# Keys' squares behind the next group's copies, gathers ahead of the attention's first key loads, one root per norm, full last key chunks

## The chip, the cores and the metric

One core of one Trainium2 chip runs the kernel. The core has a matmul engine (TensorE, PE), a vector engine (VectorE, DVE), a scalar engine (ScalarE, ACT), a general engine (GpSimd, POOL) and SyncE (SP), which here only issues DMA transfers; POOL issues DMA transfers too. Each engine runs its instructions in order and waits on semaphores for the others. The metric is the device time of one execution in microseconds (us), lower is better.

## The reference

Eight sequences of 100 tokens with 512 features (`x`) go through four layers, each added to `x`; each has its own context of 722 rows.

```python
x = x + _L0_xattn_ref(ctx_1024, _layernorm(x))     # time warping: sums of context rows along the path
x = x + _L0_ffn_ref(_layernorm(x), ...)            # 16 experts, the best 3 per token
x = x + _L1_xattn_ref(ctx_1024, _layernorm(x), mask_BxS2_bk0, ...)
x = x + _L1_ffn_ref(_layernorm(x), ...)            # 4 experts over one base product, 2 per token
```

What the change touches is the third layer. It norms its input once more, takes keys and values from the context's 722 rows and from the 100 tokens, and scales each head's query and key to unit root mean square:

```python
xn = layernorm(x, ln_x_g, ln_x_b)                  # x: the context, 722 rows
ln = layernorm(latents, ln_l_g, ln_l_b)            # latents: _layernorm(x), 100 rows
q = ln @ W_q
kv = jnp.concatenate([xn @ W_kv, ln @ W_kv], axis=1)
k, v = (kv[..., :INNER], kv[..., INNER:])          # to 8 heads of 64
qn = rmsnorm(q, q_gamma) * SCALE
kn = rmsnorm(k, k_gamma)
sim = jnp.einsum('bhid,bhjd->bhij', qn, kn)
sim = jnp.where(full_mask[:, None, None, :], sim, neg)   # tokens' keys are never masked
attn = jax.nn.softmax(sim, axis=-1)
out = jnp.einsum('bhij,bhjd->bhid', attn, v) @ W_out + b_out
```

Here `rmsnorm` divides by `max(norm / sqrt(64), 1e-8)`. The latents are a layer norm of a layer norm: with variance v and e = 1e-5, the factor of both together is 1 / sqrt(v / (v + e) + e) x 1 / sqrt(v + e).

## The kernel before

All arithmetic is in float32. A scheduler puts each engine's instructions in order, from the program's order and its own estimates, unless the program says otherwise (`tc.manual_schedule` keeps the program's own order for the engines it names, `tc.issue_after` puts instructions behind a given one).

The 800 tokens are rows in seven tiles of 128 (`NT`, the last of 32). Stages in order of time, with the span's us from the trace:

*Distances, time warping, path (0 to 403).* DVE runs the wavefront of the cost matrix, and then 100 steps of the path (L440), each over a row loaded back from `step_d`. L448 makes the selector `sel`, and `pf` (L453) on PE spreads the path over partitions. Then `pe` (L483) sums context rows (`cr`) along the path.

*Context keys and values (121 to 606, beside all that).* The context's 722 rows per sequence are six chunks of 128, in two groups of three: 16 groups, 48 chunks. `products(b, ct, c0)` (the first of two functions with that name) makes, for each chunk, `pk` and `pv` (L720, four fp32 matmuls each, of 512 columns, two passes each), ACT copies them with a scale per row to `k` (L724) and `vr` (L726), and POOL adds a bias to `k` (L725). Then, for the whole group, ACT takes 24 squares with a running sum (L737, eight heads of three chunks) and one root (L740) into `rk`. `keys` of the group before (`behind`) follows: DVE limits and inverts `rk` (L746, L747), POOL multiplies (L750), PE transposes (`ptk`, L754), ACT copies to `kt` (L755), and POOL issues the store to `k_d` (L757); the values' stores to `v_d` are issued by POOL at L728 and L733. All PSUM tiles here (`pk`, `pv`, `ptk` and those ahead of the loop) share one ring of four banks with the tag `mm`. There are two buffers of `k`, `vr` and `rk` and one of `kt`.

*Route and experts (488 to 946).* The router's products `pt`, `pl` end at 529.4, DVE computes places (with `pw` from PE in between, L571), POOL issues 21 indirect stores of rows to `xs_d` from 561.6 to 588.3, PE and DVE add the experts' output biases (`po` L673, `X` L674). Then 16 expert slots: `xr` loads, `px` transposes (L796), `xe` copy (L798), `ph` (L807), `py` (L822), and `rows_out`, whose last store to `ys_d` POOL issues at 946.55. The pools of the keys' stage are closed ahead of the experts'.

*Spill branch (near 946 to 961).* `tc.If(some > 0)` holds work for tokens that found no place. With these inputs it is not taken, but all engines meet there. `load(b)` for the attention issues, on SP, the context's keys of a sequence (`akt`, L910, 1444 KB), the mask row (`mw`, L912); ACT makes `mb` from it (L915). `early` loads two sequences ahead of the queries, and a third load comes from the attention's loop.

*Queries (961 to 1091).* For each token tile, POOL gathers three expert rows (`back`, L978, indirect, four buffers), DVE adds them (L982), then takes the statistics (L988, L989), and the norm of the norm with two roots on ACT (L992, L995) and reciprocals and products on DVE (L993 to L998), then `xn` (L1000). PE transposes (`pt` L1003), multiplies (`pqk` L1013, `apv` L1049), DVE norms per head (L1017 to L1022), PE transposes again (`apt`), ACT makes `qt` and `kl`, and SP stores `kl` to `k_d` (L1041) and loads the tokens' columns of the early keys (`tokens`, L924). From tile 2 on the first sequence's `scores` (`psc` L933) and `largest` (L943) run too.

*Attention (1091 to 1300).* A sequence has 822 keys, the 722 of the context and the 100 tokens, in seven chunks that start at `STARTS`; the sixth has 82 rows, the seventh 100 (`key_rows`). For each of the four head pairs and two groups of chunks (`KG`, four and three) PE makes `pst` (L1113), DVE adds the negated maximum (L1123), ACT takes the exponentials with the mask as a bias per row (`mk`, L1129), PE multiplies with the values (`apo` L1141), POOL adds the weights over chunks (`two`, `ws`, L1153 to L1160), PE spreads their sums (`pws` L1167) and DVE inverts (`rs` L1174). `va` holds the values (L1099, L1103, five loads a sequence).

*Last feed-forward (1300 to 1536)* on PE.

Of the kernel before, what the change touches and what calls it, by code (L numbers as in the profile page):

```python
# [33 lines left out]
MW = (S2 + 3) // 4  # L34
# [11 lines left out]
KW = S2 + KP  # L46
STARTS = (0, 128, 256, 384, 512, 640, S2)
# [11 lines left out]


def key_rows(c):
    return (*STARTS, KEYS)[c + 1] - STARTS[c]

# [6 lines left out]
def kernel(  # L70
# [47 lines left out]
    nc.vector.tensor_scalar_mul(qgs, gcol[:, 0:1], DH ** -0.5)  # L118

# [382 lines left out]
    if True:  # L502
# [178 lines left out]
        for half, dst in ((0, kbias), (1, vbias)):  # L681
            pb = kps.tile([P, D], F32, tag="mm", name="kvb")
            for dc in range(DC):
                nc.tensor.matmul(
                    pb, lncol[:, 1, dc : dc + 1].to_broadcast([P, P]), wc[:, dc, half * D : (half + 1) * D],
                    start=dc == 0, stop=dc == DC - 1,
                )
            nc.scalar.copy(dst, pb)
        pb = kps.tile([P, D], F32, tag="mm", name="kvc")
# [10 lines left out]
        for half in range(2):  # L700
            pb = kps.tile([P, D], F32, tag="mm", name="kvm")
# [7 lines left out]
        def products(b, ct, c0):  # L709

            k = kvp.tile([P, 3, D], F32, tag="k", name="k")
            vr = kvp.tile([P, 3, D], F32, tag="vr", name="vr")
            rk = kvp.tile([P, 3, NH], F32, tag="rk", name="rk")
            for c in range(c0, c0 + 3):
                rs = crstd[:, b, c : c + 1]
                pk = kps.tile([P, D], F32, tag="mm", name="pk")
                pv = kps.tile([P, D], F32, tag="mm", name="pv")
# [8 lines left out]
                nc.scalar.mul(vr[:, c - c0, :], pv, rs)  # L726
# [4 lines left out]
            if c0 > 0:  # L731
                for r0, r1 in ((0, RLAST // 16 * 16), (RLAST // 16 * 16, RLAST)):
                    nc.gpsimd.dma_start(out=v_d[b, (RC - 1) * P + r0 : (RC - 1) * P + r1, :], in_=vr[r0:r1, 2, :])  # L733
            junk = kvp.tile([P, DH], F32, tag="kjunk", name="kjunk", bufs=1)
            for c in range(3):
                for h in range(NH):
                    nc.scalar.activation(  # L737
                        junk, k[:, c, h * DH : (h + 1) * DH], AF.Square, accum_out=rk[:, c, h : h + 1]
                    )
            nc.scalar.activation(rk, rk, AF.Sqrt, scale=1.0 / DH)  # L740
            return b, c0, k, rk

        def keys(b, c0, k, rk):

# [3 lines left out]
            for c in range(3):  # L748
                kh = k[:, c, :].rearrange("p (h d) -> p h d", h=NH)
                nc.gpsimd.tensor_tensor(kh, kh, rk[:, c, :].unsqueeze(2).to_broadcast([P, NH, DH]), ALU.mult)  # L750
                ptk = kps.tile([P, D], F32, tag="mm", name="ptk")
# [8 lines left out]
        for b in range(B):  # L760
# [3 lines left out]
            for c0 in range(0, RC, 3):  # L764
                now = products(b, ct, c0)
                if behind is not None:
                    keys(*behind)
# [126 lines left out]
    if True:  # L894
# [8 lines left out]
        if True:  # L903
            ak = attn.enter_context(tc.tile_pool(name="attnk", bufs=2, side="right"))

            def load(b):

                kt = ak.tile([P, NPAIR, KW], F32, tag="akt", name="akt", bufs=3)
                nc.gpsimd.memset(kt[:, :, KEYS:], 0.0)
                nc.sync.dma_start(out=kt[:, :, :S2], in_=k_d[b, :, :, :S2])  # L910
# [3 lines left out]
                nc.gpsimd.memset(mb[:, S2:], 0.0)  # L914
                nc.scalar.activation(mb[:, :S2], mw.bitcast(U8)[:, :S2], AF.Copy, bias=-FMAX, scale=FMAX)  # L915
# [6 lines left out]
            def tokens(st):  # L922

                nc.sync.dma_start(out=st["kt"][:, :, S2:KEYS], in_=k_d[st["b"], :, :, S2:])  # L924
# [41 lines left out]
            early = [load(b) for b in range(2)]  # L966
            with tc.tile_pool(name="qkv", bufs=2, side="right") as qp:
                nc.sync.dma_start(out=wo, in_=w_out.rearrange("(c p) n -> p c n", p=P))
                nc.sync.dma_start(out=bo, in_=b_out.partition_broadcast(P))
                eps = qp.tile([P, 1], F32, name="eps", bufs=1)  # L970
                nc.gpsimd.memset(eps, EPS)
                given = 0
                for t in range(NT):
                    n = tok_rows(t)
                    cols = ds(t * P, n)
                    for k in range(TOPK):
                        back = qp.tile([P, D], F32, tag="back", name="back", bufs=4)
                        nc.gpsimd.indirect_dma_start(  # L978
# [11 lines left out]
                    rr = qp.tile([P, 4], F32, tag="rr", name="rr")  # L990
                    one, var, two, shift = (rr[:, i : i + 1] for i in range(4))
                    nc.scalar.activation(one, mv[:, 1:2], AF.Sqrt, bias=eps)  # L992
                    nc.vector.reciprocal(one, one)  # L993
                    nc.vector.scalar_tensor_tensor(var, mv[:, 1:2], one, one, ALU.mult, ALU.mult)
                    nc.scalar.activation(two, var, AF.Sqrt, bias=eps)  # L995
# [500 lines left out]
```

## Time and profile before

| what | value |
|---|---|
| median of 3 runs | 1538.27 us (1536.83 to 1538.72) |
| profiled execution, its own time | 1538.33 us |
| its span | 1536.6 us |
| mean granted TensorE clock | 0.949 |
| PE busy | 1385.6 us, 90% of the span |
| DVE, ACT, POOL busy | 684.9, 485.2, 436.1 us |
| PE busy 121 to 596 in L720 | 191.9 + 176.1 us |
| DMA | 217.78 MB, mean 142 GB/s |

The page gives busy time over the whole span; which engine sets the time differs by stage, so one reads a stage's window first, then what ended PE's idle time in it:

```profile
sum 1152.00, PE 1063.07 PEld 712.35 DVE 366.53 ACT 316.03 POOL 306.61; mean PE 75.93 PEld 50.88 DVE 26.18 ACT 22.57 POOL 21.90
```

This is the last line of the table of windows from 385 us to the end: of 1152 us PE is busy 1063, so 89 us of PE's idle time lie there. In a line of the groups, the figures after the bar are busy us and the mean ns of one instruction, then the idle us just before such an instruction, with the releaser of most of it. In a timeline line the bracket gives the idle time before and what released it.

### The profile page before, as it was taken

To read this page: it belongs to the slowest core of one execution; us is meant where nothing else is said; L and a number is where in the kernel's file an instruction comes from. 1 tells how busy PE (TensorE), PEld (TensorE's weight loads), DVE (VectorE), ACT (ScalarE), POOL (GpSimd) and SP (SyncE) were. 2 spreads that over 40 slices of the span, in tenths; PEclk is the share of its full clock that TensorE was granted. 3 is DMA by queue.
4 is the path that set the end of the run, shared out by engine and by line. 5 is a ranking of instruction groups with operands and counts; after the bars stand their busy time and mean duration, and the time that the engine had idled before them with its cause. 6 is when DMAs were issued, how large, how long until landed. Compare 5 with 4: busy or idle time off the path is not lost. (4 is left out here: it accounts for less than half of the span.)

```text
span 1536.6 us, 19541 instructions
## 1 busy us (share of the span) xinstructions
PE 1385.6 (90%) x7043; PEld 870.6 (57%) x7043; DVE 684.9 (45%) x1492; ACT 485.2 (32%) x1506; POOL 436.1 (28%) x552
## 2 busy tenths in 40 slices
PE   5979887989799998999999996499999997899998
PEld 4443333444333543899999995144476765544433
DVE  3579999799723251101100100634477773322220
ACT  3424354554522554121122221132354543200000
POOL 1014333545423356000000000600365554322210
PEclk8989899999999998899999998699899999999999
DMA  9861213542655143866567786521544420400000
GB/s 307 298 169 38 78 51 109 167 122 71 207 169 158 56 163 139 291 245 237 204 228 250 260 291 237 143 48 35 194 139 133 134 89 1 164 0 0 1 23 21
DMA packets 120857, 217.78 MB, mean 142 GB/s; under 512 B 47765, under 2 KB 49077, under 8 KB 120629
## 3 DMA queue, kind: packets, MB, share of 16 engines
q1 hardware_dynamic: 103413, 152.54, 30.9%
q0 software_dynamic: 16464, 61.44, 11.5%
q10 hardware_dynamic: 880, 2.51, 0.5%
q8 instruction: 58, 0.95, 0.3%
q14 instruction: 42, 0.34, 0.1%
HBM read 163.92 MB, written 50.86 MB: 140 GB/s over the span
## 5 line engine op out<-in xcount | busy, mean ns | idle before, releaser
L720 PE MATMUL pk<-wc,ctk 128*128 128x512 f32 x384 | 191.9, 641 | 25.8 <-ACT vr L726 22.7
L720 PE MATMUL pv<-wc,ctk 128*128 128x512 f32 x384 | 176.1, 597 | 0.0
L807 PE MATMUL ph<-xe,w1t 128*128 128x192 f32 (+4 forms) x1024 | 171.5, 314 | 1.3 <-DVE xe L798 1.3
L822 PE MATMUL py<-hT,w2t 128*128 128x192 f32 (+4 forms) x1024 | 169.7, 310 | 0.0
L807 PEld LDWEIGHTS ph<-xe,w1t 128*128 128x128 f32 x1024 | 154.4, 192 | 4.7 <-DVE xe L798 1.7
L822 PEld LDWEIGHTS py<-hT,w2t 128*128 128x128 f32 x1024 | 153.1, 191 | 1.8
L720 PEld LDWEIGHTS pk<-wc,ctk 128*128 128x128 f32 x384 | 76.9, 205 | 123.6 <-issue 92.8
L737 ACT ACTIVATE kjunk<-k 128x64 f32<-128x64 f32 x384 | 98.0, 255 | 111.3 <-POOL k L725 95.5
L811 ACT ACTIVATE hT<-ph,b1t 128x192 f32<-128x192 f32 (+4 forms) x128 | 51.8, 404 | 253.4 <-PE ph L807 253.4
L720 PEld LDWEIGHTS pv<-wc,ctk 128*128 128x128 f32 x384 | 73.1, 191 | 91.6 <-issue 88.6
L1129 ACT ACTIVATE et<-et,mk 128x200 f32<-128x200 f32 (+2 forms) x224 | 85.8, 451 | 67.2 <-DVE et L1123 67.1
L725 POOL TENSOR_TENSOR k<-k,kbias 128x512 f32<-128x512 f32 x48 | 71.9, 1503 | 99.1 <-ACT k L724 98.9
L798 DVE COPY xe<-px 128x768 f32<-128x768 f32 (+4 forms) x16 | 14.0, 875 | 185.8 <-PE ph L807 170.4
L835 POOL DMA_DIRECT2D ys_d<-yr x28 | 15.3, 547 | 285.8 <-ACT yr L834 285.8
L1356 PE MATMUL fpb<-xT,wi 128*128 128x400 f32 x256 | 91.5, 507 | 1.0 <-DVE z L1378 1.0
L1405 PE MATMUL fpo<-wot,hw 128*128 128x512 f32 x192 | 84.8, 595 | 0.0
L750 POOL TENSOR_TENSOR k<-k,rk 128x512 f32<-128x512 f32 x48 | 63.7, 1353 | 60.2 <-DVE rk L747 60.2
L440 DVE SCALAR_TENSOR_TENSOR junk<-two_i,path,C 8x735 f32<-8x735 f32 x64 | 74.1, 1157 | 9.7 <-DMA C<-step_d 7.7
L1113 PE MATMUL pst<-qt,akt 64*128 64x100 f32 x896 | 66.3, 282 | 6.8 <-DVE et L1123 6.7
L737 ACT ACTIVATION_READ_ACCUMULATOR kjunk<-k 128x1 f32 x384 | 72.0, 188 | 0.0
L1356 PEld LDWEIGHTS fpb<-xT,wi 128*128 128x128 f32 x256 | 47.0, 190 | 42.5 <-issue 9.4
L943 DVE CUSTOM_DVE_ANT_0 junk<-psc,mb 100x822 f32<-100x822 f32 x64 | 64.2, 1003 | 13.6 <-PE psc L933 13.3
(334 smaller groups left out, 2031.3 us busy)
## 6 DMA issues: line engine op xcount, KB each, us to landing
w1t<-in_w SPq DMA_DIRECT2D x16, 2048.0 KB
w2t<-in_w SPq DMA_DIRECT2D x16, 2048.0 KB
ct<-in_context_t SPq DMA_DIRECT2D x8, 1444.0 KB
ctk<-in_context_t POOLq DMA_DIRECT2D x8, 1444.0 KB
akt<-k_d SPq DMA_DIRECT2D x8, 1444.0 KB
cr<-in_context SPq DMA_DIRECT2D x8, 1280.0 KB
va<-v_d SPq DMA_DIRECT2D x8, 1280.0 KB
v_d<-vr POOLq DMA_DIRECT2D x8, 768.0 KB
```

Of the source, the lines that this page charges most:

```text
L440: nc.vector.scalar_tensor_tensor(junk, two_i1, path[:, j + 1 : j + 2], scol, ALU.is_le, ALU.mult, accum_out=path[:, j : j + 1])
L720: nc.tensor.matmul(ps, ct[:, dc, c * P : (c + 1) * P], wc[:, dc, lo : lo + D], start=dc == 0, stop=dc == DC - 1)
L725: nc.gpsimd.tensor_tensor(kc, kc, kbias, ALU.add)
L737: nc.scalar.activation(junk, k[:, c, h * DH : (h + 1) * DH], AF.Square, accum_out=rk[:, c, h : h + 1])
L750: nc.gpsimd.tensor_tensor(kh, kh, rk[:, c, :].unsqueeze(2).to_broadcast([P, NH, DH]), ALU.mult)
L807: nc.tensor.matmul(ph[:, :cap], st["w1t"][:, dc, hc * P : (hc + 1) * P], st["xe"][:, dc, :cap], start=dc == 0, stop=dc == DC - 1,)
L822: nc.tensor.matmul(py[:, dc, :cap], st["w2t"][:, hc, (2 * dh + dc) * P : (2 * dh + dc + 1) * P], st["hT"][:, hc, :cap], start=hc == 0, sto ...
L943: nc.vector.tensor_tensor_reduce(out=junk, in0=ps.rearrange("p b c -> p (b c)")[:S, :KEYS], in1=st["mb"], scale=1.0, scalar=-FMAX, op0=ALU ...
L1113: nc.tensor.matmul(ps[:, i, (c - c0) * S : (c - c0 + 1) * S], st["kt"][rows, hp, STARTS[c] : STARTS[c] + KP], qt[rows, hp, b * S : (b + 1) ...
L1129: nc.scalar.activation(et[:n, c - c0], et[:n, c - c0], AF.Exp, bias=mk[:n, b, c : c + 1])
L1356: nc.tensor.matmul(pb[:, :N2], wi[fc * P // FQ][:, dc, fc * P % FQ : fc * P % FQ + P], xT[:, dc, hh * N2 : (hh + 1) * N2], start=dc == 0, ...
L1405: nc.tensor.matmul(po[:n], hw[:, fc, t * P : t * P + n], wot[:, fc, :], start=fc == 0, stop=fc == FC - 1)
```

## The change

Five edits. (1) The squares and the root move from `products` to `keys`, which runs one group later, and each chunk's eight squares are issued behind the value copy of the same chunk of the next group. `k` gets a third buffer, `pk` and `pv` share three PSUM banks, and `ptk` has one of its own. (2) The two roots of the norm of the norm become one: 1 / sqrt(v (1 + e) + e x e) is the same factor; `eps` becomes a constant, set at the start. (3) The gathers, adds and norm of tile t + 1 come ahead of tile t's products in the program, DVE keeps the program's order there, and the first two key loads move from SP ahead of the branch to POOL's queue, behind the gathers of tiles 1 and 2. (4) The last two key chunks start at 594 and 694 and hold 128 rows each; rows that an earlier chunk has are masked, by the table the host lays out. The work per chunk is then over 128 rows throughout: values in three loads instead of five, the weights' sums in four adds instead of five, and the padding and its memset go. (5) The mask bytes cover the tokens too, so that `mb` is written by one instruction.

```diff
 KEYS = S2 + S
-MW = (S2 + 3) // 4
+MW = (S2 + S + 3) // 4
 KG = ((0, 4), (4, 7))
...
 KP, KC = 128, 7
-KW = S2 + KP
-STARTS = (0, 128, 256, 384, 512, 640, S2)
+STARTS = (0, 128, 256, 384, 512, S2 - KP, KEYS - KP)
 NCH, CW = 15, 49
...
-def key_rows(c):
-    return (*STARTS, KEYS)[c + 1] - STARTS[c]
...
+    eps = const.tile([P, 1], F32, name="eps")
+    nc.gpsimd.memset(eps, EPS * EPS)
...
-            k = kvp.tile([P, 3, D], F32, tag="k", name="k")
+            k = kvp.tile([P, 3, D], F32, tag="k", name="k", bufs=3)
             vr = kvp.tile([P, 3, D], F32, tag="vr", name="vr")
-            rk = kvp.tile([P, 3, NH], F32, tag="rk", name="rk")
+            out_of = []
             for c in range(c0, c0 + 3):
                 rs = crstd[:, b, c : c + 1]
-                pk = kps.tile([P, D], F32, tag="mm", name="pk")
-                pv = kps.tile([P, D], F32, tag="mm", name="pv")
+                pk = kps.tile([P, D], F32, tag="mm", name="pk", bufs=3)
+                pv = kps.tile([P, D], F32, tag="mm", name="pv", bufs=3)
                 for ps, lo in ((pk, 0), (pv, D)):
...
                 nc.gpsimd.tensor_tensor(kc, kc, kbias, ALU.add)
-                nc.scalar.mul(vr[:, c - c0, :], pv, rs)
+                out_of.append(nc.scalar.mul(vr[:, c - c0, :], pv, rs))
             full = 3 if c0 == 0 else 2
...
                     nc.gpsimd.dma_start(out=v_d[b, (RC - 1) * P + r0 : (RC - 1) * P + r1, :], in_=vr[r0:r1, 2, :])
+            return b, c0, k, out_of
+        def keys(b, c0, k, _, later=()):
+            rk = kvp.tile([P, 3, NH], F32, tag="rk", name="rk")
             junk = kvp.tile([P, DH], F32, tag="kjunk", name="kjunk", bufs=1)
             for c in range(3):
-                for h in range(NH):
-                    nc.scalar.activation(
-                        junk, k[:, c, h * DH : (h + 1) * DH], AF.Square, accum_out=rk[:, c, h : h + 1]
-                    )
+                with tc.issue_after(later[c].ins) if later else nullcontext():
+                    for h in range(NH):
+                        nc.scalar.activation(
+                            junk, k[:, c, h * DH : (h + 1) * DH], AF.Square, accum_out=rk[:, c, h : h + 1]
+                        )
             nc.scalar.activation(rk, rk, AF.Sqrt, scale=1.0 / DH)
-            return b, c0, k, rk
-        def keys(b, c0, k, rk):
...
                 nc.gpsimd.tensor_tensor(kh, kh, rk[:, c, :].unsqueeze(2).to_broadcast([P, NH, DH]), ALU.mult)
-                ptk = kps.tile([P, D], F32, tag="mm", name="ptk")
+                ptk = kps.tile([P, D], F32, tag="tk", name="ptk", bufs=1)
                 ptv = ptk.rearrange("p (c n) -> p c n", c=NPAIR)
...
                 if behind is not None:
-                    keys(*behind)
+                    keys(*behind, later=now[-1])
                 behind = now
...
-            def load(b):
-                kt = ak.tile([P, NPAIR, KW], F32, tag="akt", name="akt", bufs=3)
-                nc.gpsimd.memset(kt[:, :, KEYS:], 0.0)
-                nc.sync.dma_start(out=kt[:, :, :S2], in_=k_d[b, :, :, :S2])
+            def load(b, queue=nc.sync):
+                kt = ak.tile([P, NPAIR, KEYS], F32, tag="akt", name="akt", bufs=3)
+                queue.dma_start(out=kt[:, :, :S2], in_=k_d[b, :, :, :S2])
                 mw = ak.tile([S, MW], I32, tag="mw", name="mw")
...
                 mb = ak.tile([S, KEYS], F32, tag="mb", name="mb")
-                nc.gpsimd.memset(mb[:, S2:], 0.0)
-                nc.scalar.activation(mb[:, :S2], mw.bitcast(U8)[:, :S2], AF.Copy, bias=-FMAX, scale=FMAX)
+                nc.scalar.activation(mb, mw.bitcast(U8)[:, :KEYS], AF.Copy, bias=-FMAX, scale=FMAX)
                 return dict(b=b, kt=kt, mb=mb)
...
-                nc.sync.dma_start(out=st["kt"][:, :, S2:KEYS], in_=k_d[st["b"], :, :, S2:])
+                nc.sync.dma_start(out=st["kt"][:, :, S2:], in_=k_d[st["b"], :, :, S2:])
...
-            early = [load(b) for b in range(2)]
+            early = []
             with tc.tile_pool(name="qkv", bufs=2, side="right") as qp:
...
                 nc.sync.dma_start(out=bo, in_=b_out.partition_broadcast(P))
-                eps = qp.tile([P, 1], F32, name="eps", bufs=1)
-                nc.gpsimd.memset(eps, EPS)
                 given = 0
-                for t in range(NT):
+                def gathered(t):
                     n = tok_rows(t)
-                    cols = ds(t * P, n)
                     for k in range(TOPK):
                         back = qp.tile([P, D], F32, tag="back", name="back", bufs=4)
-                        nc.gpsimd.indirect_dma_start(
+                        got = nc.gpsimd.indirect_dma_start(
                             out=back[:n], out_offset=None, in_=ys_d,
...
                     nc.vector.bn_aggr(mv, st)
-                    rr = qp.tile([P, 4], F32, tag="rr", name="rr")
-                    one, var, two, shift = (rr[:, i : i + 1] for i in range(4))
-                    nc.scalar.activation(one, mv[:, 1:2], AF.Sqrt, bias=eps)
-                    nc.vector.reciprocal(one, one)
-                    nc.vector.scalar_tensor_tensor(var, mv[:, 1:2], one, one, ALU.mult, ALU.mult)
-                    nc.scalar.activation(two, var, AF.Sqrt, bias=eps)
+                    rr = qp.tile([P, 2], F32, tag="rr", name="rr")
+                    two, shift = rr[:, 0:1], rr[:, 1:2]
+                    nc.scalar.activation(two, mv[:, 1:2], AF.Sqrt, scale=1.0 + EPS, bias=eps)
                     nc.vector.reciprocal(two, two)
-                    nc.vector.tensor_tensor(two, two, one, ALU.mult)
                     nc.vector.scalar_tensor_tensor(shift, mv[:, 0:1], -1.0, two, ALU.mult, ALU.mult)
...
                     nc.vector.tensor_scalar(xn, X[:, t, :], two, shift, ALU.mult, ALU.add)
+                    return xn, got
+                hand = tc.manual_schedule(engines={mybir.EngineType.DVE})
+                hand.__enter__()
+                xns = {0: gathered(0)}
+                for t in range(NT):
+                    n = tok_rows(t)
+                    cols = ds(t * P, n)
+                    if t + 1 < NT:
+                        xns[t + 1] = gathered(t + 1)
+                    if t < 2:
+                        with tc.issue_after(xns[t + 1][1].ins):
+                            early.append(load(t, nc.gpsimd))
+                    xn = xns.pop(t)[0]
                     pt = aps.tile([P, D], F32, tag="tr", name="pt", bufs=1)
...
                             largest(st, hp, i, ps)
+                hand.__exit__(None, None, None)
                 for part in range(3):
...
                 nc.sync.dma_start(
-                    out=va[:, : KC - 2, :], in_=v_d[b, : STARTS[KC - 2], :].rearrange("(c p) d -> p c d", p=KP)
-                )
-                for c, r0, r1 in ((KC - 2, 0, 80), (KC - 2, 80, key_rows(KC - 2)), (KC - 1, 0, 96), (KC - 1, 96, S)):
-                    nc.sync.dma_start(out=va[r0:r1, c, :], in_=v_d[b, STARTS[c] + r0 : STARTS[c] + r1, :])
+                    out=va[:, : KC - 2, :], in_=v_d[b, : (KC - 2) * KP, :].rearrange("(c p) d -> p c d", p=KP)
+                )
+                for c in (KC - 2, KC - 1):
+                    nc.sync.dma_start(out=va[:, c, :], in_=v_d[b, STARTS[c] : STARTS[c] + KP, :])
                 st["va"] = va
...
                 for c in range(c0, c1):
-                    n = key_rows(c)
-                    nc.scalar.activation(et[:n, c - c0], et[:n, c - c0], AF.Exp, bias=mk[:n, b, c : c + 1])
+                    nc.scalar.activation(et[:, c - c0], et[:, c - c0], AF.Exp, bias=mk[:, b, c : c + 1])
                 return et
...
                 for c in range(c0, c1):
-                    n = key_rows(c)
                     for i in range(2):
...
                         nc.tensor.matmul(
-                            st["po"][i * DH : (i + 1) * DH, hp, :], st["va"][:n, c, h * DH : (h + 1) * DH],
-                            et[:n, c - c0, i, :], start=c == 0, stop=c == KC - 1,
+                            st["po"][i * DH : (i + 1) * DH, hp, :], st["va"][:, c, h * DH : (h + 1) * DH],
+                            et[:, c - c0, i, :], start=c == 0, stop=c == KC - 1,
                         )
...
                 two = st["two"]
-                nc.gpsimd.tensor_tensor(two[:, 0], two[:, 0], et[:, 0], ALU.add)
+                nc.gpsimd.tensor_tensor(two, two, et[:, 0:2], ALU.add)
                 nc.gpsimd.tensor_tensor(ws[:, hp], two[:, 0], two[:, 1], ALU.add)
-                for c in (1, 2):
-                    n = key_rows(KG[1][0] + c)
-                    nc.gpsimd.tensor_tensor(ws[:n, hp], ws[:n, hp], et[:n, c], ALU.add)
+                nc.gpsimd.tensor_tensor(ws[:, hp], ws[:, hp], et[:, 2], ALU.add)
...
     mask[:, :S2] = np.ascontiguousarray(f["mask_BxS2_bk0"]).view(np.uint8)
-    keys = np.ones((B, KC + 1, KP), np.uint8)
-    keys[:, : KC - 1].reshape(B, -1)[:, :S2] = mask[:, :S2]
+    mask[:, S2:KEYS] = 1
+    keys = np.zeros((B, KC + 1, KP), np.uint8)
+    for c, s in enumerate(STARTS):
+        new = max(STARTS[c - 1] + KP if 0 < c < KC - 1 else S2 if c else 0, s) - s
+        keys[:, c, new:] = mask[:, s + new : s + KP]
     a_t = np.zeros((D, P), np.float32)
...
```

## The prediction

> **What bounds the kernel now.** I read the busy tenths first: TensorE (PE) is busy 1385.6 of 1536.6 us, so only PE's idle stretches and what runs while PE has nothing can give time back. Then the costliest groups, PE's waits from 60 to 640 us, and the timeline round each of three holes.
>
> ```profile
> L720 PE MATMUL pk<-wc,ctk 128*128 128x512 f32 x384 | 191.9, 641 | 25.8 <-ACT vr L726 22.7
> ...
> L737 ACT ACTIVATE kjunk<-k 128x64 f32<-128x64 f32 x384 | 98.0, 255 | 111.3 <-POOL k L725 95.5
> ...
> L737 ACT ACTIVATION_READ_ACCUMULATOR kjunk<-k 128x1 f32 x384 | 72.0, 188 | 0.0
> ```
>
> A chunk's eight squares occupy ACT for 8 x (255 + 188) ns less their overlap; the timeline has them 0.38 us apart, 3.05 us a chunk. They wait for GpSimd's bias add (95.5 us in all), and ACT runs in order, so the copies that free PSUM stand behind them. PE pays for it:
>
> ```profile
> PE pk L720 <- ACT vr L726: 22.7, 9, 3.8
> PE ptk L754 <- ACT vr L726: 8.8, 4, 4.5
> ...
> PE pe L483 <- DMA cr<-in_context: 6.5, 2, 3.3
> PE ptk L754 <- ACT k L724: 4.2, 5, 0.9
> ```
>
> First hole: these waits make PE late for the path. The columns of the next view are start, duration, engine, line.
>
> ```profile
> 402.91 1.63 DVE L448 COPY sel<-ident 8x1024 f32<-8x1024 f32 x1
> ...
> 411.60 2.02 PE L453 MATMUL pf<-path,sel 8*128 8x101 f32 x16
> ```
>
> The selector is ready at 404.54; PE reaches it 7.1 us later, still working off keys and values.
>
> Second hole: the last keys before the experts. The windows give PE 59.71 busy of 60 us from 530 to 590, and then:
>
> ```profile
> 590.00:617.00 27.00, 18.05 (x52) 8.40 (x50) 5.82 (x11) 17.53 (x87) 14.93 (x16) 0.72 0.41 142
> ```
>
> The columns are the window, its length, busy time of PE, weight loads, DVE, ACT, POOL, the granted clock, DMA share, GB/s. Nine us are idle and part of the rest runs at a low clock: GpSimd was issuing the 21 indirect puts until 588.3, so bias adds were late, then 48 squares ran on ACT from 589.6 to 606.8 without a break, then `rk`, the residual adds and the first expert (`ph` at 616.88).
>
> Third hole: the join after the spill branch, and the first norm.
>
> ```profile
> 950.00:955.00 5.00, 0.00 (x0) 0.00 (x0) 0.00 (x0) 0.64 (x1) 0.00 (x0) 0.51 1.01 332
> 955.00:960.00 5.00, 0.00 (x0) 0.00 (x0) 0.00 (x0) 0.98 (x2) 0.00 (x0) 0.50 0.96 355
> ```
>
> ```profile
> 960.74 0.10 POOL L971 MEMSET eps<- 128x1 f32 x1 [13.65 <-DMA akt<-k_d]
> 961.56 1.14 POOL L978 DMA_INDIRECT back<-ys_d,seen  x1 [0.72 <-issue]
> ...
> 968.29 0.75 DVE L982 SCALAR_TENSOR_TENSOR X<-back,gk,X 128x512 f32<-128x512 f32 x1 [0.99 <-DMA back<-ys_d,seen]
> ...
> 979.08 1.09 PE L1003 MATMUL pt<-ident,xn 128*128 128x128 f32 x4 [33.49 <-DVE xn L1000]
> ```
>
> Every engine stands still while three 1444 KB loads of attention keys, issued from 944.66 to 947.68, use the whole DMA. Only then does the first gather start, and PE gets its first operand 33.5 us after its last work.
>
> **Part 1, squares behind copies, up to the path.** The same 384 squares, bias adds, products and transposes run. In the changed kernel's instruction order a group's squares stand behind the next group's value copy, and by then their bias add is long done: the 95.5 us wait of ACT goes. One product is eight passes, 3.43 us from start to start (404.64 to 408.07 in the timeline), and a chunk's transposes 0.5 (12 passes in 1.47). ACT's work per chunk is 0.67 + 0.67 + 3.05 + 0.69 (the `kt` copy) = 5.1 us against PE's 2 x 3.43 + 0.5 = 7.35 us, so it fits. The new order has 32 chunks of products and 24 transposes of keys ahead of `pf`, before it was 33 `pk`, 32 `pv` and 27. The new PE work from 121 us is 32 x 6.86 + 12 = 231.5 us of the 282 us to 402.8, so PE has slack. VectorE, 143.19 of 150 us busy from 120 to 270, sets the pace there. So `pf` comes right after `sel`, about 404.7: **-7**.
>
> **Up to the route.** Between `pf` and the last router product the old order has 14.5 products of 3.43 us and 9 transposes of 0.5 us, 54.2 us; the new one has 12.5 and 9, 47.4 us. That is 6.8 us, and with perhaps 2 us of the 6.5 us `cr` wait the last router product comes near 514 instead of 529.4: 15 earlier. But 11.8 us of key work are now behind it: 9.5 `pk`, 10 `pv` and 15 transposes, 19.5 x 3.43 + 7.5 = 74.4 us, against 8 + 8.5 and 12, 62.6 us before.
>
> **Up to the experts.** From last router product to `ph` the old kernel took 87.5 us: 62.6 of keys, about 15 of hole, 10 of other. The new one needs 74.4 + 10 = 84.4 us without a hole, so `ph` at 514 + 84.4 = 598.4, or 18 earlier at best (eight transposes move behind the first `ph`, worth 4 us of the sum, but not free). Against it: the transposes have one PSUM bank instead of four, so four in a row are paced by transpose, copy (0.69), and multiply (1.35); and `pw` stands behind 22 us of key work where it was 16.9, so DVE waits some 5 us and the puts start about 2.6 us later against the router. I take 3 to 6 us for these. **-12**, bounds 0 (the tail's chain is only shifted) and -18.
>
> **Part 2, the join.** The two early loads leave SP's list ahead of the branch and go on POOL's queue behind the gathers; the third is issued by SP after the branch. `eps` is a constant, so its memset goes too. What remains ahead is the last expert write, issued 946.55 and 0.54 long. A gather lands about 2.8 us after its issue ends (965.50 less 962.70); the write by that row at 949.9; from release to gather is 0.82 (960.74 to 961.56). First gather 950.7: **-10.9**. Four mask loads now stand ahead of the branch; two of them took 4.72 us of SP at 955.2, so four could hold SP to 945.6 + 9.4 = 955 and the gather to 956: bound -5.6. I take the upper value, as the mask loads before (0.36 and 1.04) were short.
>
> **First norm.** From the third add's end, 969.04, to `pt` at 979.08 are 10.0 us, since DVE interleaves later tiles' adds (0.75 each) and the norm makes two trips to ACT. With the hand order and one root: statistics 0.69 + 0.16, trip and root about 0.9, reciprocal 0.15, shift 0.2, `xn` 0.52, start 0.3: 2.9 us. **-7**; the third load, 4.3 us of DMA at 332 GB/s, now runs beside the first gathers and can delay them by about 2: bound -5.
>
> Each load moved costs POOL an issue: the context loads from POOL took 0.773 to 0.837 us, the key loads from SP 0.530 to 0.700. Behind them stand the gathers of tiles 2 and 3, not needed for 15 us (PE's pace per tile); 0. If a load is late the tokens' columns and the first `psc` (1020.49, 7.7 us after its token load was issued at 1012.82) wait: 0 to +5, I take **+2**, also for DVE's hand order, where adds wait in line for gathers ahead of the query work.
>
> The Trainium skill speaks against this step: "DMA: Bandwidth & Descriptors", section "Issuing engine by pattern", gives simple loads to Sync and only indirect ones to GpSimd, and its Specifications put the first byte at about 1 us against 0.6. By the page the two loads would cost an estimated 0.8 us more, with the sum at +2.8 instead of +2; the trace shows only the longer issue.
>
> **Part 3, full last chunks.** The product count is unchanged. GpSimd per half pair runs 1.04 + 1.04 + 0.61 + 0.61 = 3.3 us instead of 1.04 + 4 x 0.61 = 3.48; `pws` waited for it 4.4 us in all from 1091 to 1300. Values need 3 loads a batch instead of 5; memsets of 0.2 us go. **-0.5**, bounds +1 and -3 (the wait gone but 1.4).
>
> **Sum.** 1538.33 (this execution: span 1536.6 and 1.7 round it, 0.06 from the runs' median 1538.27) - 12 - 10.9 - 7 + 2 - 0.5 = **1509.9, call it 1510**. The expert, QKV and last feed-forward stages are PE-bound (328.28 of 329 us from 617 to 946) and only shift.
>
> **Rivals.**
> *The key work moves but gives nothing* (20%). For: 11.8 us of it go behind the router, where the route's DVE chain and puts decide. Against: PE stood idle there 9 of 27 us. Then 1510 + 12 = **1522**.
> *The gathers gain little* (16%): the mask loads and the third load hold them, and the first `psc` waits 5: -5.6 - 5 + 5 = -5.6 instead of -15.9, so **1520**. For: SP's 4.72 us. Against: the whole-DMA windows were keys.
> *Slower: the one transpose bank* (9%). PE in order waits at each key chunk until ACT has copied the last one out from behind its eight squares. Slack until the path is (282 - 231.5)/32 = 1.6 us a chunk; a loss of 2 us a chunk makes `pf` 0.4 x 30 = 12 late (it was 7 late before), takes 16 x 2 = 32 after it, and leaves the other 10 of the key work and the join's 16: 1538 + 12 - 7 + 32 - 10 - 16 = **1549**. It is slower from about 1.7 us a chunk on. Against: in the new order one product of 3.43 us stands between most transposes, over the 3.05 of squares.
> *It does not do what it says* (3%): buffers tie the early loads to the old time, PE's order hides the rest: 1538.
>
> **Numbers.** The forecast has 51%. Its own terms at their ends give 1500 to 1528, so the range is 1498 to 1530 and holds both milder rivals. About 0.2% (3 us) is what a measurement tells from no change: faster 0.87, same 0.03, slower 0.10, with 1% for other losses.
>
> **What would show it.** Right: `pf` within 2 us of `sel`; the squares' wait for `k` L725 near zero; `ph` near 605; first gather near 951 and its `pt` near 10 us behind; no 13.7 us wait for `akt`. Wrong: PE waits on `kt` or `ptk`, mask loads between the last write and the first gather, or a wait of `psc` on `akt` over 5 us.

## The result, and the profile after

The changed kernel takes 1557.09 us (median of 4 runs, 1555.63 to 1558.75) against 1537.97 before: ratio 1.0124, 95% interval 1.0108 to 1.0140. It is 19 us slower where I had forecast 28 us faster. The span of its profiled execution is 1553.9 us, 17.3 over that of before, and the tables below follow those 17.3.

Start of the same work in both traces, in us:

| point | before | after | after less before |
|---|---|---|---|
| `pf`, the path's spread | 411.6 | 401.3 | -10.3 |
| last router product `pl` | 529.3 | 512.7 | -16.6 |
| first expert product `ph` | 616.9 | 606.8 | -10.1 |
| first store to `ys_d` | 654.3 | 656.2 | +1.9 |
| last store to `ys_d` | 946.5 | 947.4 | +0.9 |
| first gather | 961.6 | 952.8 | -8.8 |
| first query transpose `pt` | 979.1 | 965.3 | -13.8 |
| `pbo`, end of the queries | 1092.2 | 1110.5 | +18.3 |
| first product of the last layer `fpb` | 1318.8 | 1336.1 | +17.3 |

Nearly every step gains what it was to gain, and two places give it back: the first expert slot takes 12.0 us (-10.1 to +1.9), and the query stage takes 32.1 (-13.8 to +18.3).

The costliest groups of the page after, to be set beside those of before (columns as there):

```profile
L719 PE MATMUL pk<-wc,ctk 128*128 128x512 f32 x384 | 188.0, 631 | 3.1 <-POOL wc L707 3.1
...
L742 ACT ACTIVATE kjunk<-k 128x64 f32<-128x64 f32 x384 | 97.8, 255 | 9.8
```

The 95.5 us that the squares waited for the bias adds are gone, and with them PE's 22.7 us in front of `pk`. But most of PE's waits have only moved. From 121 to 402 us, about up to `pf`, PE waited in the kernel before (us in total, times, longest):

```profile
PE pk L720 <- ACT vr L726: 22.7, 9, 3.8
PE ptk L754 <- ACT vr L726: 8.8, 4, 4.5
PE ptk L754 <- ACT k L724: 3.3, 4, 0.9
```

and after:

```profile
PE ptk L755 <- POOL k L751: 27.7, 6, 10.2
PE pf L452 <- DVE sel L447: 4.6, 1, 4.6
```

That is 34.8 us before and 32.3 after. The transposes now wait for POOL's multiply (L751), and the multiply for `rk` (98.0 us of its idle time on the page), which comes out of the later squares.

PE in a steady tile of the query stage after, from the timeline (start, duration, engine, line, operation; in brackets the idle time before it and its releaser):

```profile
1023.50 3.60 PE L1020 MATMUL pqk<-wkv,xT 128*128 128x512 f32 x8
1027.02 1.62 PE L932 MATMUL psc<-akt,qt 64*100 64x512 f32 x4
1028.58 0.66 PE L1010 MATMUL pt<-ident,xn 128*128 128x128 f32 x4
1032.85 1.94 PE L1037 MATMUL apt<-ident,qn 128*128 128x128 f32 x8 [3.62 <-DVE qn L1029]
1034.72 3.06 PE L932 MATMUL psc<-akt,qt 64*100 64x512 f32 x4
1037.71 6.06 PE L1056 MATMUL apv<-wkv,xT 128*100 128x512 f32 x8
```

Between `pqk` and the transposes `apt` of the same tile lies the query norm (ACT squares, DVE reduces, ACT takes the root, DVE inverts and multiplies). PE has 2.2 us of other work for it and then stands for 3.62 us. What follows runs slowly: `apt` 1.94 us instead of 1.04, four `psc` 3.06 instead of 1.62, eight `apv` 6.06 instead of 3.60. The wait comes in four of the seven tiles:

```profile
PE apt L1037 <- DVE qn L1029: 14.5, 4, 3.6
```

In the kernel before, the same `apv` stood ahead of `apt` and covered the norm:

```profile
1033.12 3.60 PE L1013 MATMUL pqk<-wkv,xT 128*128 128x512 f32 x8
1036.56 3.60 PE L1049 MATMUL apv<-wkv,xT 128*100 128x512 f32 x8
1040.09 1.62 PE L933 MATMUL psc<-akt,qt 64*100 64x512 f32 x4
1041.64 0.66 PE L1003 MATMUL pt<-ident,xn 128*128 128x128 f32 x4
1042.13 1.04 PE L1030 MATMUL apt<-ident,qn 128*128 128x128 f32 x8
```

Why the order changed, as I read it: DVE is kept in the program's order from here on, and the program subtracts the values' bias (`avr`, L1061) behind the query norm. A product `apv` ahead of `apt` would have no reader yet, so the scheduler puts it behind. E1 and E5 test this.

The first expert slot after, PE again:

```profile
606.83 5.35 PE L808 MATMUL ph<-xe,w1t 128*128 128x256 f32 x24
612.01 0.60 PE L755 MATMUL ptk<-ident,k 128*128 128x128 f32 x4
...
618.85 0.60 PE L755 MATMUL ptk<-ident,k 128*128 128x128 f32 x4
...
631.42 1.09 PE L755 MATMUL ptk<-ident,k 128*128 128x128 f32 x4 [4.81 <-ACT kt L756]
633.37 1.09 PE L755 MATMUL ptk<-ident,k 128*128 128x128 f32 x4 [0.87 <-ACT kt L756]
635.23 5.08 PE L823 MATMUL py<-hT,w2t 128*128 128x256 f32 x12 [0.78 <-ACT kt L756]
```

Six of the 48 chunks' transposes now stand among the expert products; before, none did (the last ran at 612.5, ahead of the first `ph` at 616.9). They take 4.64 us and bring waits of 0.15, 0.61, 4.81, 0.87 and 0.78, together 7.22: 11.9 of the 12.0 us. Before, PE was busy in all 37.4 us of this slot. The long one is the one buffer of `kt`, whose next copy waits for the store of the group before (the copy shows 5.50 us idle, released by the store to `k_d`).

The join after:

```profile
952.81 1.14 POOL L975 DMA_INDIRECT back<-ys_d,seen  x1 [4.84 <-DMA mw<-in_mask]
954.26 1.05 POOL L975 DMA_INDIRECT back<-ys_d,seen  x1 [0.30 <-issue]
```

The wait of 13.65 us for `akt` is 4.84 us for the mask now.

### The profile page after: what moved, and what is told of

It is laid out like the page before. It is cut to its first block, busy times and chain, and to the rows that moved or that the text cites. A ratio compares the mean times of both kernels' runs of the same rounds, so it can differ in the third digit from the quotient of the medians.

```text
span 1553.9 us, 19452 instructions
## 1 busy us (share of the span) xinstructions
PE 1401.1 (90%) x7043; PEld 877.4 (56%) x7043; DVE 685.4 (44%) x1471; ACT 486.2 (31%) x1499; POOL 418.0 (27%) x506
## 4 chain that ended last, share of the span: by engine, by line
PE 61%; DVE 16%; DMA 11%; issue 7%; ACT 2%; SPq 1%; POOL 1%; another core or an unknown queue 1%; DVEq 0%; ACTq 0%; POOLq 0%
PE py L823 10%; PE ph L808 9%; PE fpb L1360 6%; PE fpo L1409 5%; PE psc L932 4%; DMA cr<-in_context 4%; PE pqk L1020 3%; PE pst L1121 3%; DVE C L394 3%; PE pv L719 3%; PE pk L719 2%; PE apv L1056 2%; DMA ct<-in_context_t 2%; PE apo L1147 2%; PE py L1190 2%
## 5 line engine op out<-in xcount | busy, mean ns | idle before, releaser
L719 PE MATMUL pk<-wc,ctk 128*128 128x512 f32 x384 | 188.0, 631 | 3.1 <-POOL wc L707 3.1
L1136 ACT ACTIVATE et<-et,mk 128x200 f32<-128x200 f32 x224 | 85.8, 451 | 66.7 <-DVE et L1131 66.7
L751 POOL TENSOR_TENSOR k<-k,rk 128x512 f32<-128x512 f32 x48 | 58.7, 1249 | 122.5 <-DVE rk L748 98.0
L724 POOL TENSOR_TENSOR k<-k,kbias 128x512 f32<-128x512 f32 x48 | 66.7, 1419 | 79.3 <-ACT k L723 79.3
L439 DVE SCALAR_TENSOR_TENSOR junk<-two_i,path,C 8x735 f32<-8x735 f32 x64 | 78.4, 1225 | 6.7 <-DMA C<-step_d 4.6
L827 DVE COPY yT<-py 128x384 f32<-128x384 f32 (+4 forms) x32 | 16.5, 516 | 133.8 <-PE py L823 133.8
```

Of the source, the lines that this page charges most:

```text
L439: nc.vector.scalar_tensor_tensor(junk, two_i1, path[:, j + 1 : j + 2], scol, ALU.is_le, ALU.mult, accum_out=path[:, j : j + 1])
L719: nc.tensor.matmul(ps, ct[:, dc, c * P : (c + 1) * P], wc[:, dc, lo : lo + D], start=dc == 0, stop=dc == DC - 1)
L724: nc.gpsimd.tensor_tensor(kc, kc, kbias, ALU.add)
L1136: nc.scalar.activation(et[:, c - c0], et[:, c - c0], AF.Exp, bias=mk[:, b, c : c + 1])
```

## The experiments

Each kernel ran beside the kernel before on the same chip; ratios are to that, with 95% intervals.

**E1. VectorE's order left to the scheduler.** Only this differs from the changed kernel:

```diff
-                hand = tc.manual_schedule(engines={mybir.EngineType.DVE})
+                hand = nullcontext()
```

> The changed kernel with VectorE's hand-written order in the query stage left to the scheduler; all else kept. Theory A (the hand order puts the query norm ahead of the values' bias subtraction, so PE's apv products, 3.6 us a tile, stand behind apt instead of covering the norm; each tile then pays 3.62 us of idle and some 4 us at half clock): the query stage from the first pt to pbo falls from 145 us to about 113 to 118, the wait of apt on qn goes, time 1525 to 1532. Theory B (the gathers are the brake: POOL's back waited 67 us for DVE's adds, and two key loads stand in its queue): the waits only move, time above 1545.

1524.01 us, ratio 0.9905 (0.9889 to 0.9922): 33 us faster than the changed kernel and faster than the one before. From the first `pt` to `pbo` it takes 108.5 us against 145.2, and the wait of `apt` on `qn` is gone. By itself this does not clear POOL's gathers, which come earlier too (the last starts at 995.9 us here, at 1049.0 in the changed kernel); E5 does.

**E2. The keys' part alone**, on the kernel before (functions `products` and `keys`, the three banks and the one of `ptk`, all as in the change).

> The kernel before with only the keys' part of the change (squares behind the next group's copies, third k buffer, three banks and one for ptk). Theory A (pf and the first ph come 10 us earlier, but the deferred transposes and their single kt buffer, which waits for its store, cost the same in the first expert slot): pf near 401, first ph near 607, first py near 635, end 1537 to 1540. Theory B (the keys' part is a gain and only the other parts lose): end 1526 to 1530.

1545.03 us, ratio 1.0037 (1.0023 to 1.0051): slower by about 6 us, more than I expected of it. `pf` 400.9, first `ph` 610.7, first `py` 641.0, last expert store 953.6 against 946.5. So the first slot gives back more than the 10.7 us gained at `pf`; PE's wait on `kt` is 4.62 us here too.

**E3. The changed kernel without the keys' part.**

> The changed kernel with the keys' part undone, the rest kept. Theory A: the keys' part is worth nothing, so 1555 to 1559. Theory B (it gains its 10 us through to the end): 1565 to 1570. Theory C (it costs by itself, through the single transposing bank): below 1552.

1558.11 us, ratio 1.0133 (1.0109 to 1.0158), against 1.0124 with it: in the changed kernel the keys' part is worth nothing either way. Why it costs 6 us by itself (E2) and nothing here was not tried.

**E4. The full last chunks alone**, with the mask bytes over the tokens.

> The kernel before with only the full last key chunks (and the mask bytes over the tokens that go with them). My step: 0.5 us less, bounds -3 and +1: 1535 to 1539. Rival: the wider exponentials and the third add of 128 rows hold POOL's sums, or one load of 128 rows more per chunk holds the values: 1541 or more.

1540.17 us, ratio 1.0001 (0.9985 to 1.0016): nothing to be seen. The interval reaches 2.4 us to either side, so the forecast of -0.5 could not be told from none.

**E5. The values' products ahead of the query norm, hand order kept.** The block is moved, not changed:

```diff
+                    while given < B and (given + 1) * S <= t * P + n:
+                        pv = aps.tile([P, D], F32, tag="po", name="apv", bufs=1)
...
+                        given += 1
                     sq = qp.tile([P, 2, D], F32, tag="asq", name="asq", bufs=1)
...
-                    while given < B and (given + 1) * S <= t * P + n:
...
-                        given += 1
                     if t < 2:
                         tokens(early[t])
```

> The changed kernel, VectorE's hand order kept, but the block with apv and avr moved in the program from behind the key stores to just behind pqk, so that avr precedes the query norm on DVE and apv precedes apt on PE. Theory A (PE's uncovered query norm is the loss, through the place of apv): the 3.62 us wait of apt on qn goes, a steady tile takes 15 to 16 us instead of 23 to 28, pt to pbo 115 to 125 us, time 1525 to 1535. Theory B (keeping DVE in order is itself the loss, whatever PE does: adds wait for gathers, later work behind them): the query stage stays over 135 us, time above 1545.

1528.90 us, ratio 0.9945 (0.9925 to 0.9965). The tile in its timeline:

```profile
1035.90 3.60 PE L1020 MATMUL pqk<-wkv,xT 128*128 128x512 f32 x8
1039.42 1.62 PE L932 MATMUL psc<-akt,qt 64*100 64x512 f32 x4
1040.98 0.65 PE L1010 MATMUL pt<-ident,xn 128*128 128x128 f32 x4
1042.18 3.68 PE L1024 MATMUL apv<-wkv,xT 128*100 128x512 f32 x8 [0.55 <-ACT xT L1012]
1045.69 1.04 PE L1048 MATMUL apt<-ident,qn 128*128 128x128 f32 x8
1046.66 1.62 PE L932 MATMUL psc<-akt,qt 64*100 64x512 f32 x4
```

The same 3.6 us of `apv` now lie where PE stood, and nothing behind them is slow. From `apt` to `apt` it is 15.9 us (1029.84 to 1045.69), in the changed kernel 23.2 (1009.66 to 1032.85). The window from 1010 to 1070, first after, then E5 (busy us of PE, weight loads, DVE, ACT, POOL; granted clock; DMA share; GB/s):

```profile
1010.00:1070.00 60.00, 51.89 (x113) 22.09 (x112) 24.38 (x45) 9.64 (x20) 5.58 (x5) 0.76 0.17 43
```

```profile
1010.00:1070.00 60.00, 58.03 (x165) 24.08 (x163) 30.19 (x55) 14.86 (x30) 5.60 (x5) 1.00 0.24 55
```

In the same 60 us the profile has 113 matmul records for the one and 165 for the other, and the granted clock is 0.76 against 1.00. So DVE in program order is no loss of that size by itself; the place of `apv` on PE, which followed from it, was. Nor are the gathers the brake: their last starts at 1036.0 here, 40 us later than in E1, and yet the stage from `pt` to `pbo` takes 116.0 us. Some 5 us remain between E5 and E1.

**E6. Gathers ahead, one root, full chunks; no keys' part, DVE free.**

> The changed kernel without the keys' part and with DVE left to the scheduler: gathers ahead, one root, full chunks. Theory A (the keys' part costs 3 to 6 us and the start of the attention gains about 20): 1517 to 1521, and the first ph back at about 617. Theory B (the keys' part gives something once the query stage is mended): 1526 to 1532.

1524.67 us, ratio 0.9918 (0.9894 to 0.9942). This lies between my two expectations and equals E1 within the intervals. The profile gives `ph` at 617.0, first gather 951.6, `pbo` 1078.9, so 13.3 us are gained from the join and the queries, and none from the keys.

**E7. As E6 with the two roots again.**

> As the run with gathers ahead and without the keys' part, but with the two roots of the norm of the norm as before. The trip to ACT and back is paid once before the first pt: Theory A: about 2 to 3 us later at the first pt and the same at the end, 1519 to 1524. Theory B (the one root is most of the gain, since the norm's small operations stand between later tiles' adds): 6 us or more slower than that run.

1523.46 us, ratio 0.9909 (0.9885 to 0.9932): no difference from E6. The first `pt` comes 16.0 us after the first gather instead of 15.2, and that 0.8 us is not found at the end.

**E9. As E6 with the early key loads on SP ahead of the branch again**, `early = [load(b) for b in range(2)]`.

> As the run with gathers ahead and without the keys' part (1524.7), but with the two early key loads on SP ahead of the branch again. Theory A (the join is the gain: engines wait there for the loads): first gather back to 960 or later, 9 to 10 us slower, 1532 to 1535. Theory B (the gain is the order of gathers and norm; the loads would have been absorbed): under 1527.

1537.85 us, ratio 0.9998 (0.9988 to 1.0007): 13.2 us slower than E6, and no gain at all over the kernel before. Its waits and its timeline at the join:

```profile
POOL back L973 <- DMA mw<-in_mask: 15.0, 1, 15.0
```

```profile
961.61 1.14 POOL L973 DMA_INDIRECT back<-ys_d,seen  x1 [15.03 <-DMA mw<-in_mask]
...
974.78 1.08 PE L1005 MATMUL pt<-ident,xn 128*128 128x128 f32 x4 [29.71 <-DVE xn L991]
```

The 15 us are put down to the mask load, which is the last thing that SP issued there (954.55, 5.33 us for two), behind three key loads from 944.15 on. With one root the first `pt` is still 4.3 us earlier than before, but the first `psc` is at 1021.8 against 1020.5 before and `pbo` at 1092.7 against 1092.2: that lead is gone before the attention. Without the move of the loads the other edits at the start gain nothing; the move without them was not run.

**E8. The last group's `kt` from the ring of `vr`**, on E1:

```diff
-            kt = kvp.tile([P, NPAIR, 3 * P], F32, tag="kt", name="kt", bufs=1)
+            kt = kvp.tile([P, NPAIR, 3 * P], F32, tag="kt" if later else "vr", name="kt", bufs=1 if later else None)
```

> The changed kernel with DVE left to the scheduler and the last group's kt taken from the ring of vr, so that its copies don't wait for the store of the group before. Theory A (4.8 us of PE's 8.1 us of waits in the first expert slot are the one kt buffer): the wait of 4.8 us of ptk on kt goes, first py 5 us earlier than 639.5, end 1518 to 1521. Theory B (slot 0 is set by ACT's squares and the multiplies of the last group): the wait takes another name and the end stays at 1523 to 1526.

1522.23 us, ratio 0.9912 (0.9882 to 0.9941); against E1's 0.9905 the time doesn't tell them apart. The traces do:

```profile
632.07 0.63 PE L755 MATMUL ptk<-ident,k 128*128 128x128 f32 x4 [0.87 <-ACT kt L756]
633.57 0.63 PE L755 MATMUL ptk<-ident,k 128*128 128x128 f32 x4 [0.87 <-ACT kt L756]
634.97 10.22 PE L823 MATMUL py<-hT,w2t 128*128 128x256 f32 x39 [0.78 <-ACT kt L756]
```

The wait of 4.8 us is gone, the transposes that followed it take 0.63 instead of 1.09 us, and `py` starts 4.5 us earlier than in E1.

**E10. Products and transposes in one ring of four banks again**, squares behind the next group's copies as in the change, on E1.

> The changed kernel with DVE left to the scheduler and the products and transposes of the keys in one ring of four PSUM banks again, squares still behind the next group's copies. Theory A (my rival: the single transposing bank costs): first py some 3 us earlier than 639.5, the 0.87 us waits of ptk on kt gone, end 1519 to 1522. Theory B (the bank is hidden, only the kt store was not): within 2 us of 1524.

1633.07 us, ratio 1.0621 (1.0597 to 1.0645): neither of my expectations, 109 us slower than E1. Its PE waits from 60 to 700 us, and a window after its first `ph` (575.1):

```profile
PE ptk L755 <- POOL k L751: 90.4, 16, 23.1
```

```profile
640.00:740.00 100.00, 75.25 (x190) 36.37 (x191) 1.93 (x8) 52.50 (x226) 30.18 (x32) 0.86 0.14 52
```

PE now waits for the multiplies, 90.4 us in 16 waits up to 700 us. As I read it, these wait for squares that stand behind the next group's copies, and in one ring the waiting transposes hold the banks that those copies' products need. What is shown is the end: 15 chunks of products and 19 of transposes are left behind the first `ph` in the built order, and the first `py` starts at 743.5. So with the late squares a bank of their own for the transposes is worth 109 us.

**E11. The last two groups' bias adds on VectorE**, on E6:

```diff
-                nc.gpsimd.tensor_tensor(kc, kc, kbias, ALU.add)
+                eng = nc.vector if 2 * b + c0 // 3 >= 14 else nc.gpsimd
+                eng.tensor_tensor(kc, kc, kbias, ALU.add)
```

> As the run with gathers ahead and without the keys' part, but the bias adds of the last two groups of keys are on DVE, which is idle while GpSimd issues the puts. Theory A (PE's 9 idle us from 590 to 617 come from squares that wait for bias adds behind the puts): squares done before the puts end, first ph 5 to 8 us earlier than 617, end 1517 to 1521. Theory B (the expert's row loads or the residual adds set the first ph): ph within 2 us, end 1523 to 1526.

1513.34 us, ratio 0.9843 (0.9827 to 0.9860), 11 us faster than E6. The first `ph` is 6.7 us earlier (610.3), the last expert store 7.4, `pbo` 9.0. In the window from 590 to 617 ACT is busy 7.56 us, where E6 had 17.56:

```profile
590.00:617.00 27.00, 19.47 (x70) 11.49 (x69) 5.82 (x8) 7.56 (x26) 8.02 (x10) 0.81 0.69 226
```

So the bias adds behind GpSimd's puts held the first `ph`. The hole is not closed: from 580 us to the first `ph` PE still waits 7.5 us, 6.2 of them for the experts' rows (`xr`). Where the rest of the 11 us, behind the experts, comes from was not tried.

**E12. The changed kernel with E1's, E8's and E11's edits.**

> The changed kernel with DVE left to the scheduler, the last kt in the ring of vr, and the last two groups' bias adds on DVE. If the keys' part and the bias move remove the same hole: within 3 us of the run with vr's ring (1522). If they add up: 1514 to 1518.

1507.88 us, ratio 0.9821 (0.9798 to 0.9844): 30 us faster than the kernel before and 49 faster than the changed one. The first `ph` is at 598.8 and the last expert store at 933.9, against 610.3 and 939.3 in E11: with its last `kt` in the ring of `vr`, the keys' part brings 5 us.

## Why the prediction was wrong

*The query stage.* The step that failed is the "+2, also for DVE's hand order". I counted the adds that wait in line on DVE, and did not read what the hand order does to PE's order, though the trace of before had the query norm's chain and the `apv` that covered it. The runs showed +32.1 us: in four tiles 3.62 us of idle each, and up to 0.90 + 1.44 + 2.46 = 4.8 us by which PE's passes take longer at a lower clock, at most 4 x 8.4 = 33.7. E1 and E5 take it away in two ways. I had given this wait no price at all, and a stall costs more here than its idle time.

*The keys.* Up to the first `ph` the times held: `pf` at once after `sel` (401.29, `sel` done at 401.21), last `pl` 512.7 where I had 514, `ph` 606.8 where I had 605. The step that failed is the next one, that the experts "only shift" and that the transposes moved behind `ph` are worth 4 us "but not free". They took 4.64 us and brought 7.22 us of waits, 6.46 of them on `kt`, a sign of being wrong that I had named; and the -12 became +0.9 at the last expert store. The reason for them held less well: I let PE's waits go with ACT's, and 27.7 us came back as waits of `ptk` on the multiply. An earlier `pf` was no gain by itself: PE came late to it before because it worked off keys, and in the changed kernel it stands idle 4.59 us for `sel` with 4.9 us less of key work done. Work on the bounding engine that is put off has to be paid where that engine has no idle time.

*The join.* From the last expert store to the first gather it is 5.4 us instead of 15.0: -9.6 where I had -10.9; four mask loads took SP 4.96 us, between my two bounds. E9 shows that without this move nothing is gained.

*The first norm.* From first gather to first `pt` 12.5 us instead of 17.5: -5.0, at my lower bound: the adds began 7.5 us after the first gather's start (960.34 against 952.81), before 3.9 us, with the third key load issued at 951.03 beside the gathers. E7 shows that the root itself is worth under 1 us. With DVE's order free the same stretch takes 15.2 us (E6) and 15.3 (E1), so some 2.8 of the 5.0 us came with the hand order, which costs far more behind it. In E9 a first `pt` that is 4.3 us earlier is worth nothing at the end.

*The chunks.* -0.5 expected; E4 can't tell it from nothing (ratio 1.0001); from `pbo` to `fpb` it is 225.6 us instead of 226.6.

*The sum.* The profiled execution took 1555.63 us, 45.7 over the forecast. To rounding, the query stage accounts for 30.1 of them (+32.1 for +2), the keys for 12.9 (+0.9 for -12), the first norm for 2.0 and the join for 1.3, and the attention gives 0.5 back. The prediction also added its bounds wrongly: with 0, -5.6, -5, +5 and +1 the upper end is 1533.7 and not 1528. The result lies far above both.

*The rivals.* Slower I had laid to the single transposing bank; E10 shows the opposite: without that bank the change, with DVE's order free, loses 109 us. "The key work moves but gives nothing" was right for its part and had 20%; no rival that I named stood in the query stage. The rule of the Trainium skill's page "DMA: Bandwidth & Descriptors", section "Issuing engine by pattern", which gives simple loads to Sync, was not followed here: on SP ahead of the branch the two loads cost 13.2 us (E9 against E6), on POOL behind the gathers an issue of 0.82 and 0.80 us in the changed kernel. These runs change the place along with the queue, and no run has the loads on SP behind the gathers; so they price the place and say nothing against the rule.

## What to carry to other kernels

Fixing the order of one engine changes the order of all others: before it is costed at a few waits, the built order of the bounding engine has to be read for what no longer covers a latency, and a gap on PE (here 3.62 us) is to be priced with what the clock can take behind it. A step that makes the bounding engine reach a point earlier is a gain only if no work was put off to do so; count the work left behind the point. And when all engines meet at a branch, the bulk loads ahead of it can be on the path, whatever they are for.

## What was not expected of the hardware

After a gap of 3.62 us PE worked slowly for some 10 us. This is the changed kernel's window from 1033 to 1042, with the columns of the windows above:

```profile
1033.00:1042.00 9.00, 9.00 (x17) 3.93 (x18) 0.30 (x1) 1.26 (x2) 0.00 (x0) 0.50 0.23 52
```

PE is busy throughout and the granted clock is 0.50. In windows of 1 us the clock is 1.00 up to 1032, 0.50 from 1033 to 1042 and 1.00 again from 1043, so PE, back at work at 1032.85, waited nearly 10 us for its full clock. The rows fit: 1.94 + 3.06 us for passes that take 1.04 + 1.62, and then, if slow passes take twice their time, 2 x (6.06 - 3.60) = 4.9 us of the eight `apv`. The Trainium skill's page "TensorE: Matmul & The Clock Gate", section "HAM oscillation — how this bites in real kernels", warns of idle gaps over about 3.4 us; this case's gaps of 3.62 agree with it, and those of 0.55 to 0.88 us in E5 left the clock at 1.00. The same page's section "What's actually happening" puts the return to full rate at one or more busy windows of about 3.4 us; here it took nearly three times that.

The length of a gap alone does not decide it here. Ahead of the first expert PE waited 2.24 us (`px` for `xr`) and then 0.87 in E8, and 3.05 us and then 0.87 in the changed kernel. What follows, first E8, then the changed kernel:

```profile
608.00:614.00 6.00, 5.36 (x15) 4.50 (x16) 1.25 (x3) 4.31 (x21) 2.76 (x3) 0.50 1.05 369
604.00:614.00 10.00, 9.13 (x54) 8.12 (x55) 2.00 (x3) 9.37 (x48) 3.81 (x4) 1.00 0.99 335
```

The shorter wait was followed by a clock of 0.50, the longer one by 1.00. No run here shows what decides it.
